# A sampled-convolution stream with another spacing of its stages: products 6 units ahead, copies 4 slots behind, 15 accumulators, 13 gather buffers

## The chip, the cores and the metric

The kernel runs on one core of a Trainium2 chip. The metric is the device time of one execution in microseconds (us); the median of the shown runs stands for a kernel. Engines are named as in the profile: PE (TensorE matmul), PEld (its weight loads), DVE (VectorE), ACT (ScalarE), POOL (GpSimd), SP (SyncE).

## What is computed

The input x has shape (2, 256, 128, 128), in float32. Two layers follow each other, each added to its input:

```
x = x + deform_conv(group_norm(x))      # layer 0
x = x + expert_conv(group_norm(x))      # layer 1
# deform_conv: a 3x3 convolution gives, for each pixel and each of 9 taps, an offset (dy, dx) and a mask;
# each tap samples x bilinearly at its moved position: four corners times four weights, times the mask;
# out = einsum('bckhw,ock->bohw', sampled, w_conv)   with c = o = 256, k = 9
# expert_conv: for 8 experts a 1x3 conv to 8 channels, then a 3x1 conv to 256, summed with probs
```

The part that matters here is the sampling of layer 0: 2 images x 128 rows x 9 taps = 2304 row samples of 128 pixels by 256 channels, and the products with `w_conv`.

## The kernel before

The head loads image 0, takes its norm and writes a table to device memory in which one line of 2 KB holds a pixel and the one below it, all 256 channels of each; two neighbouring lines, 4 KB in one piece, are the four corners of a cell. After the head comes the **stream**, which takes nearly all of the time, and then a tail with the second layer of image 1.

The stream works in **units**. A unit is one output row and one tap: 128 pixels on the partitions, four corners of 256 channels. Four rows (`CR`) form a chunk of 36 units (4 rows x 9 taps); two chunks form a group of 72 units, for which the sampling positions and weights are worked out together. There are 2304 units. The order of all instructions is written out by hand: a loop over **slots** `s` issues, in each slot, steps of several units at fixed distances. No scheduler moves anything; each engine runs its own instructions in the order in which the loop issues them, and waits where an operand or a buffer is not ready. In one slot:

- POOL issues `gather(s + GA)` (L567): one indirect DMA of 128 pieces of 4 KB, 512 KB, into a buffer `g` of the pool `gather`, which has `GA` buffers. The buffer is free once the last add of unit `s` has run.
- ACT runs `product(s + LP)` (L577): first corner times its weight into a new accumulator `acc` (pool `acc`).
- DVE runs three adds (L583): corners 1 and 2 of unit `s + 1` and corner 3 of unit `s`. After its corner 3 the unit's gather buffer is free.
- PE runs `apply_tap(s - LM)` (L608): one 128x512 product of the finished samples `sm` with `wcv` into `po`; four such steps, at the four units of a tap, make one tap complete. Two matmuls are issued for each of them.
- PE runs `turn(s - TL)` (L593): the accumulator of unit `s - 1` is transposed into `ptr` in PSUM (two halves). A `ptr` tile holds two units; there are three tiles. The accumulator is then free.
- ACT runs, in every other slot, `keep(s - TL - KL)` (L601): it copies a `ptr` tile of two units into `sm` (three tiles of four units).

At the end of a chunk DVE adds `po` to x (`residual`, L617) two slots after the last `apply_tap` of its half, then takes statistics (L621). `po` has one buffer for each half, so the first `apply_tap` of the next chunk waits for this add.

Other pieces lie in the same slots: the offset convolution of the group to come (`pu`, L335, and `om`, L350, on PE; its copy on ACT, its position arithmetic on DVE), over half of image 0's slots the table of image 1 (L667 and L677 on ACT, transposes on PE, loads and stores from SP), and over image 1's slots the second layer of image 0 (L766, L773, L832, L847, L856). Their slots are counted from the group's first unit; those of the offset pieces also from `GA`, those of the end of a chunk from `LM`.

Of the kernel before, what the change touches and what calls it, by code (L numbers as in the profile page):

```python
# [62 lines left out]
UPG = UPC * CPG  # L63
UPI = UPG * NG
UNITS = B * UPI
GA = 15
LP = 3
TL = 1
KL = 2
LM = 8  # L70
XB, XR = 3, 5


# [1 line left out]
def layers(ctx, tc, x, w_om, b_om, w_cv, b_cv, w_in, w_out, probs, out):  # L75
# [75 lines left out]
    def norm_pieces(stats, small, psum, tag, name):  # L151
        mean = cp.tile([P, NH], F32, name=f"mean_{name}")
        rstd = cp.tile([P, NH], F32, name=f"rstd_{name}")
        shift = cp.tile([P, NH], F32, name=f"shift_{name}")
        mv = small.tile([P, NH, 2], F32, tag="mv", name=f"mv_{name}")
        own = small.tile([P, NH], F32, tag="own", name=f"own_{name}")
        g = gavg.rearrange("p a b -> p (a b)")
        ps = {}

        def average(what):  # L160
            ps[what] = psum.tile([P, 512], F32, tag=tag, name=f"ps_{what}_{name}")
            nc.tensor.matmul(ps[what][:, :NH], lhsT=g, rhs=own, start=True, stop=True)

        def aggregate(h):
            nc.vector.bn_aggr(mv[:, h], stats[:, h].rearrange("p c s -> p (c s)"))

        pieces = [
            lambda: aggregate(0),
            lambda: aggregate(1),
            lambda: nc.vector.tensor_copy(own, mv[:, :, 0]),  # L170
            lambda: average("mean"),
            lambda: nc.vector.tensor_copy(mean, ps["mean"][:, :NH]),

            lambda: nc.vector.tensor_sub(own, own, mean),
            lambda: nc.vector.tensor_mul(own, own, own),
            lambda: nc.vector.tensor_add(own, own, mv[:, :, 1]),
            lambda: average("var"),
            lambda: nc.scalar.activation(rstd, ps["var"][:, :NH], AF.Sqrt, bias=eps),
            lambda: nc.vector.reciprocal(rstd, rstd),
            lambda: nc.vector.scalar_tensor_tensor(shift, mean, -1.0, rstd, ALU.mult, ALU.mult),  # L180
        ]
        return (mean, rstd, shift), pieces
# [100 lines left out]
    def pool(stack, name, bufs, **kw):  # L283
        return stack.enter_context(tc.tile_pool(name=name, bufs=bufs, reuse_waits="tile", **kw))
# [17 lines left out]
    stream = ExitStack()  # L302
# [217 lines left out]


    gp = pool(stream, "gather", GA)
    ap = pool(stream, "acc", 8)
    sp = pool(stream, "sampled", 3)
    st = pool(stream, "stat", 1)
    p_o = pool(stream, "p_o", 1, space=PSUM)
# [12 lines left out]
    def put(slot, piece, opens=False):  # L539
        sched[slot].append(piece)  # L540
        if opens:
            opened.add(slot)
# [20 lines left out]
    def gather(u):  # L563
        b, ci, k, r = unit(u)
        idx, _, rr, k = sample_of(u)
        gt = gp.tile([P, 2 * CELL], F32, tag="gt", name=f"g_{b}_{ci}_{k}_{r}")
        nc.gpsimd.indirect_dma_start(  # L567
            out=gt[:], out_offset=None, in_=tables[b][:, :],
            in_offset=bass.IndirectOffsetOnAxis(ap=idx[:, rr, k : k + 1], axis=0),
        )  # L570
        gts[u] = gt

    def product(u):
        b, ci, k, r = unit(u)
        _, wt, rr, k = sample_of(u)
        acc = ap.tile([P, C], F32, tag="acc", name=f"acc_{b}_{ci}_{k}_{r}")
        nc.scalar.activation(acc, gts[u][:, 0:C], AF.Copy, scale=wt[:, 0, rr, k : k + 1])  # L577
        accs[u] = acc

    def add(u, q):  # L580
        _, wt, rr, k = sample_of(u)
        gt = gts[u] if q < 3 else gts.pop(u)
        nc.vector.scalar_tensor_tensor(  # L583
            accs[u], gt[:, q * C : (q + 1) * C], wt[:, q, rr, k : k + 1], accs[u], ALU.mult, ALU.add
        )

    def turn(u):
        b, ci, k, r = unit(u)
        if r % 2 == 0:
            pts[u // 2] = p_t.tile([P, NH, 2 * W], F32, tag="t", name=f"ptr_{b}_{ci}_{k}_{r}")  # L590
        acc = accs.pop(u)
        for h in range(NH):
            nc.tensor.transpose(  # L593
                pts[u // 2][:, h, (r % 2) * W : (r % 2 + 1) * W], acc[:, h * P : (h + 1) * P], ident
            )

    def keep(u):
        b, ci, k, r = unit(u)
        if r == 1:
            sms[u // CR] = sp.tile([P, NH, N], F32, tag="sm", name=f"sm_{b}_{ci}_{k}")  # L600
        nc.scalar.copy(sms[u // CR][:, :, (r - 1) * W : (r + 1) * W], pts.pop(u // 2))  # L601

    def apply_tap(u):
        b, ci, k, i = unit(u)
        m, h = divmod(i, NH)
        if k == 0 and h == 0:
            pos_[b, ci, m] = p_o.tile([P, N], F32, tag=f"o{m}", name=f"po_{b}_{ci}_{m}")
        nc.tensor.matmul(  # L608
            pos_[b, ci, m], lhsT=wcv[:, h, k, m * P : (m + 1) * P], rhs=sms[u // CR][:, h],
            start=(k == 0 and h == 0), stop=(k == K2 - 1 and h == NH - 1),  # L610
        )
# [15 lines left out]
    def table_beside(b):  # L627
# [10 lines left out]
        def load_group(g, what):  # L638
            xt = held[what, "g", g] = x_tile(b, g, what)
            nc.sync.dma_start(xt, xv[:, :, g * GN : (g + 1) * GN])  # L640
            if g < XB:
                xts[b, g] = xt
# [42 lines left out]
        for j in range(NCH):  # L685
# [3 lines left out]
            elif i == 0:  # L689

                slot = max(slot, UPG * (g - NG + XR + 1) + LM + 12)
                put(slot, lambda g=g: load_group(g, "xs"))
# [9 lines left out]
        pieces, first_rows, last_rows = offset_pieces(b, oc, p_m, "m")  # L702
        at = UPI - 68 - GA - UPG + 46
        for n, piece in enumerate((*pieces[:2], *[None] * 3, *pieces[2:], first_rows)):
            if piece:
                put(at + 2 * n, piece)
        assert at + 2 * n < UPI - 68 - GA + 55
        put(UPI + UPI // 2, last_rows)
# [189 lines left out]
    def result_stats_of(b):  # L898
        stats1[b] = st.tile([P, NH, NCH, 6], F32, tag=f"stats{b}", name=f"stats1_{b}")

    result_stats_of(0)
    for G in range(B * NG):
# [6 lines left out]
        if (b, g) != (0, 0):  # L909
            for n, piece, opens in offsets_of(b, g):  # L910
                put(slot - 68 - GA + n, piece, opens)
    norms1 = [None] * B
    tabled = table_beside(1)
    assert tabled < UPI - GA - 16
    put(UPI - 16, sides.close)
    put(UPI, lambda: result_stats_of(1))
    slot = UPI + LM + 10
    norms1[0], pieces = norm_pieces(stats1[0], st, p_m, "m", "1_0")
# [12 lines left out]
    def when(u):  # L931
        return 0 <= u < UNITS

    s = min(sched)
    end = UNITS + LM
    while s < end or any(t >= s for t in sched):
        if when(s + GA):
            gather(s + GA)
        if when(s + LP):
            product(s + LP)  # L940

        order = [(s + 1, 1), (s, 3), (s + 1, 2)] if s in opened else [(s + 1, 1), (s + 1, 2), (s, 3)]
        for u, q in order:
            if when(u):
                add(u, q)
        if when(s - LM):
            u = s - LM
            apply_tap(u)
# [7 lines left out]
        if when(s - TL):  # L956
            turn(s - TL)
        if when(s - TL - KL) and (s - TL - KL) % 2 == 1:
            keep(s - TL - KL)
        for piece in sched.pop(s, ()):  # L960
# [67 lines left out]
```

## Time and profile before

| what | us |
|---|---|
| median of 3 runs (4056.10, 4062.48, 4065.21) | 4062.48 |
| the profiled execution, its own time | 4155.75 |
| its span, first to last instruction | 4154.0 |
| first and last gather issued | 156.2 and 3959.0 |

The profiled execution is 2.3% above the median of the runs; sums made in the profile are made against 4155.75 us. The stream's 2304 units take 3803 us between the first and the last gather, 1.65 us each. In a row of the profile, "idle before" is time in which that engine did nothing before such an instruction, with what ended most of it; a line "A <- B" in the list of waits adds up the idle time of A that the profile puts down to B.

### The profile page before, as it was taken

To read this page: it belongs to the slowest core of one execution; us is meant where nothing else is said; L and a number is where in the kernel's file an instruction comes from. 1 tells how busy PE (TensorE), PEld (TensorE's weight loads), DVE (VectorE), ACT (ScalarE), POOL (GpSimd) and SP (SyncE) were. 2 spreads that over 40 slices of the span, in tenths; PEclk is the share of its full clock that TensorE was granted. 3 is DMA by queue.
4 is the path that set the end of the run, shared out by engine and by line. 5 is a ranking of instruction groups with operands and counts; after the bars stand their busy time and mean duration, and the time that the engine had idled before them with its cause. 6 is when DMAs were issued, how large, how long until landed. Compare 5 with 4: busy or idle time off the path is not lost.

```text
span 4154.0 us, 51837 instructions
## 1 busy us (share of the span) xinstructions
PE 3497.9 (84%) x14044; PEld 1870.3 (45%) x14044; DVE 3442.1 (83%) x8066; ACT 1837.6 (44%) x3883; POOL 2335.4 (56%) x2388
## 2 busy tenths in 40 slices
PE   3588888888878888888889888889988889888889
PEld 2443434444444444444444444444545445444444
DVE  6488988888888887889788888888888888888887
ACT  2244444445444554444444444444444444444432
POOL 0356666656665666656566555556656556555531
PEclk9699999999999999989999999999999999999999
DMA  9999999999999999999889999999999999988835
GB/s 360 358 358 370 356 371 346 342 335 366 372 372 378 389 394 387 376 361 369 315 329 349 333 344 345 334 350 340 363 339 356 331 349 354 351 320 327 327 118 193
DMA packets 419516, 1425.46 MB, mean 343 GB/s; under 512 B 41582, under 2 KB 45338, under 8 KB 419098
## 3 DMA queue, kind: packets, MB, share of 16 engines
q0 software_dynamic: 331776, 1208.11, 78.0%
q1 hardware_dynamic: 87450, 214.04, 13.6%
q8 instruction: 114, 1.87, 0.2%
q14 instruction: 176, 1.44, 0.1%
HBM read 1298.20 MB, written 123.78 MB: 342 GB/s over the span
## 4 chain that ended last, share of the span: by engine, by line
PE 42%; DVE 25%; DMA 12%; issue 11%; another core or an unknown queue 6%; ACT 3%; POOL 1%; POOLq 1%; SPq 0%; ACTq 0%; DVEq 0%
PE po L608 23%; DVE acc L583 19%; DMA g<-table,cidx 9%; PE ptr L593 7%; PE pu L335 3%; PE pe L832 2%; PE ph L766 2%; DMA table<-hpx 2%; ACT acc L577 1%; PE ph L811 1%; PE pe L847 1%; DVE stats L621 1%; POOL g L567 1%; DVE x L617 1%
## 5 line engine op out<-in xcount | busy, mean ns | idle before, releaser
L583 DVE SCALAR_TENSOR_TENSOR acc<-g,wt,acc 128x256 f32<-128x256 f32 x6912 | 2961.8, 480 | 466.3 <-ACT acc L577 325.7
L567 POOL DMA_INDIRECT g<-table,cidx x2304 | 2284.5, 992 | 1530.9 <-DVE acc L583 556.5
L608 PE MATMUL po<-sm,wcv 128*128 128x512 f32 x4608 | 2502.1, 625 | 301.5 <-ACT sm L601 130.8
L601 ACT COPY sm<-ptr 128x512 f32<-128x512 f32 x1152 | 672.7, 584 | 1933.6 <-PE ptr L593 1096.3
L593 PEld LDWEIGHTS ptr<-idp,acc 128*128 128x128 f32 x4608 | 626.4, 146 | 1622.3 <-issue 1075.9
L593 PE MATMUL ptr<-idp,acc 128*128 128x128 f32 x4608 | 935.2, 286 | 195.4 <-ACT sm L601 76.3
L577 ACT ACTIVATE acc<-g,wt 128x256 f32<-128x256 f32 x2304 | 1060.1, 506 | 43.2 <-DMA g<-table,cidx 29.7
L608 PEld LDWEIGHTS po<-sm,wcv 128*128 128x128 f32 x4608 | 753.4, 199 | 375.3 <-ACT sm L601 160.4
L335 PE MATMUL pu<-wus,x 128*128 128x81 f32 (+2 forms) x1448 | 270.1, 313 | 7.8 <-issue 6.7
L335 PEld LDWEIGHTS pu<-wus,x 128*128 128x128 f32 x1448 | 216.8, 200 | 10.3 <-issue 6.9
L617 DVE SCALAR_TENSOR_TENSOR x<-po,bcv,x 128x512 f32<-128x512 f32 x116 | 86.3, 744 | 59.6 <-PE ptr L593 21.8
L832 PE MATMUL pe<-h,wout 128*128 128x256 f32 (+1 forms) x384 | 127.2, 461 | 1.0 <-DVE xc L856 1.0
L766 PE MATMUL ph<-xcn,win 128*64 128x254 f32 (+1 forms) x768 | 98.1, 403 | 4.6 <-issue 4.6
L856 DVE TENSOR_TENSOR xc<-pe,xc 128x512 f32<-128x512 f32 x76 | 49.8, 683 | 44.3 <-PE pe L847 20.0
L350 PE MATMUL om<-u,idp 128*128 128x216 f32 x192 | 56.0, 375 | 33.1 <-ACT u L344 30.7
L832 PEld LDWEIGHTS pe<-h,wout 128*128 128x128 f32 x384 | 67.9, 193 | 33.7 <-issue 30.1
L621 DVE BATCH_NORM_STATS2 stats<-x 128x6 f32<-128x512 f32 x116 | 79.2, 683 | 0.1
L766 PEld LDWEIGHTS ph<-xcn,win 128*64 128x64 f32 x768 | 55.9, 145 | 37.6 <-issue 16.6
L847 PE MATMUL pe<-h,wout 64*128 64x128 f32 (+1 forms) x752 | 70.1, 322 | 1.3 <-issue 1.3
L504 DVE COPY hpx<-hpt 128x512 f32<-128x512 f32 x32 | 21.1, 687 | 57.2 <-DMA table<-hpx 47.0
L799 DVE TENSOR_TENSOR v<-xcn 128x512 f32<-128x512 f32 x96 | 65.9, 744 | 1.8 <-ACT xcn L786 1.8
L847 PEld LDWEIGHTS pe<-h,wout 64*128 64x128 f32 x752 | 52.1, 187 | 27.4 <-issue 18.8
(115 smaller groups left out, 1019.3 us busy)
## 6 DMA issues: line engine op xcount, KB each, us to landing
g<-table,cidx POOLq DMA_INDIRECT x2304
table<-tpx SPq DMA_DIRECT2D x32, 1024.0 KB
table<-hpx SPq DMA_DIRECT2D x15, 2048.0 KB
x<-in_x_dram SPq DMA_DIRECT2D x29, 1024.0 KB
out_dram<-xc SPq DMA_DIRECT2D x38, 512.0 KB
x<-x SPq DMA_DIRECT2D x16, 1024.0 KB
out_dram<-x SPq DMA_DIRECT2D x26, 512.0 KB
xs<-in_x_dram SPq DMA_DIRECT2D x22, 512.0 KB
```

Source lines behind the costliest of these rows:

```text
L335: nc.tensor.matmul(held["ps", j][:, lo:hi], lhsT=xt[:, h, r * W : (r + 1) * W], rhs=w[:, lo - i + 2 : hi - i + 2], start=(i == 2 and h == ...
L567: nc.gpsimd.indirect_dma_start(out=gt[:], out_offset=None, in_=tables[b][:, :], in_offset=bass.IndirectOffsetOnAxis(ap=idx[:, rr, k : k + ...
L577: nc.scalar.activation(acc, gts[u][:, 0:C], AF.Copy, scale=wt[:, 0, rr, k : k + 1])
L583: nc.vector.scalar_tensor_tensor(accs[u], gt[:, q * C : (q + 1) * C], wt[:, q, rr, k : k + 1], accs[u], ALU.mult, ALU.add)
L593: nc.tensor.transpose(pts[u // 2][:, h, (r % 2) * W : (r % 2 + 1) * W], acc[:, h * P : (h + 1) * P], ident)
L601: nc.scalar.copy(sms[u // CR][:, :, (r - 1) * W : (r + 1) * W], pts.pop(u // 2))
L608: nc.tensor.matmul(pos_[b, ci, m], lhsT=wcv[:, h, k, m * P : (m + 1) * P], rhs=sms[u // CR][:, h], start=(k == 0 and h == 0), stop=(k == K ...
L617: nc.vector.scalar_tensor_tensor(v, pos_.pop((b, ci, m)), bcv[:, m : m + 1], v, ALU.add, ALU.add)
L621: nc.vector.bn_stats(stats1[b][:, m, ci], xts[b, ci // CPG][:, m, at_ : at_ + N])
L766: nc.tensor.matmul(o[:, :, to], lhsT=win[:, h, tap], rhs=pairs[:, t, :, of], start=(q == 0), stop=(q == 5),)
L832: nc.tensor.matmul(ps[t][:, m], lhsT=wout[:, 2 * t, m * P : (m + 1) * P], rhs=hs[ci], start=(banks or m == 0), stop=False,)
L847: nc.tensor.matmul(ps[t][:, m, to], lhsT=wout[half, 1, m * P : (m + 1) * P], rhs=hs[c][half, of], start=False, stop=(banks or m == NH - 1) ...
```

## The change

Five constants change: `GA`, `LP`, `KL`, `LM` and the number of buffers in the pool `acc`. Nothing is added or taken away: the same instructions run on the same engines, at other distances from each other.

```diff
-GA = 15
-LP = 3
+GA = 13
+LP = 6
 TL = 1
-KL = 2
-LM = 8
+KL = 4
+LM = 9
...
     gp = pool(stream, "gather", GA)
-    ap = pool(stream, "acc", 8)
+    ap = pool(stream, "acc", 15)
```


A gather buffer takes 4 KB of each partition and an accumulator 1 KB, so the two pools together take 67 KB in place of 68 KB. What the new distances mean for one unit u, counted in slots:

| step of unit u | slot before | slot after |
|---|---|---|
| gather issued (POOL), waits for the last add of unit | u - 15, unit u - 15 | u - 13, unit u - 13 |
| product (ACT), waits for the transposes of unit (its accumulator) | u - 3, unit u - 8 | u - 6, unit u - 15 |
| adds (DVE) | u - 1 and u | u - 1 and u |
| transposes (PE) | u + 1 | u + 1 |
| copy out of PSUM (ACT), u odd | u + 3 | u + 5 |
| its product with `wcv` (PE) | u + 8 | u + 9 |

Between the issue of a gather and the product that reads it lie 12 slots before and 7 after. Between the copy of the last two units of a tap and the tap's first `apply_tap` lie 2 slots before and 1 after. A `ptr` tile is wanted again by the transposes of the pair three pairs on; its copy lies 3 slots ahead of them before and 1 after.

## The prediction

> **What bounds the kernel now.** I read the page's part 1 and the groups first, then the list of waits, then one stall in the timeline, and last counted positions from the trace's start and end times.
>
> ```profile
> PE 3497.9 (84%) x14044; PEld 1870.3 (45%) x14044; DVE 3442.1 (83%) x8066; ACT 1837.6 (44%) x3883; POOL 2335.4 (56%) x2388
> L583 DVE SCALAR_TENSOR_TENSOR acc<-g,wt,acc 128x256 f32<-128x256 f32 x6912 | 2961.8, 480 | 466.3 <-ACT acc L577 325.7
> L608 PE MATMUL po<-sm,wcv 128*128 128x512 f32 x4608 | 2502.1, 625 | 301.5 <-ACT sm L601 130.8
> L601 ACT COPY sm<-ptr 128x512 f32<-128x512 f32 x1152 | 672.7, 584 | 1933.6 <-PE ptr L593 1096.3
> L593 PE MATMUL ptr<-idp,acc 128*128 128x128 f32 x4608 | 935.2, 286 | 195.4 <-ACT sm L601 76.3
> L577 ACT ACTIVATE acc<-g,wt 128x256 f32<-128x256 f32 x2304 | 1060.1, 506 | 43.2 <-DMA g<-table,cidx 29.7
> ```
>
> No engine is full: DVE and PE are both near 84%, and each idles some 500 us in the stream. ACT has less than half its time in work, yet DVE waits 325.7 us for ACT's products, and ACT itself stands 1933.6 us ahead of its PSUM copies. The products hardly wait for gathered data (29.7 us). So ACT is not slow and the data is not late; ACT stands at a copy, and products that it could have made lie behind it in its queue. The waits say it in pairs:
>
> ```profile
> ACT sm L601 <- PE ptr L593: 1096.3, 610, 9.5
> POOL g L567 <- DVE acc L583: 556.5, 794, 6.1
> DVE acc L583 <- ACT acc L577: 325.7, 79, 13.5
> PEld ptr L593 <- DVE acc L583: 263.1, 441, 2.1
> PEld po L608 <- ACT sm L601: 160.4, 59, 8.0
> PE po L608 <- ACT sm L601: 130.8, 53, 7.8
> PE po L608 <- DVE x L617: 90.0, 51, 5.4
> PE ptr L593 <- ACT sm L601: 76.3, 25, 5.0
> ```
>
> DVE's waits are few and long (79, 4.1 us each); PE's for DVE are many and short (441). One stall, in the timeline:
>
> ```profile
> 1148.39 0.59 ACT L601 COPY sm<-ptr 128x512 f32<-128x512 f32 x1 [5.75 <-PE ptr L593]
> 1148.87 0.91 ACT L577 ACTIVATE acc<-g,wt 128x256 f32<-128x256 f32 x2
> 1150.23 0.38 PE L593 MATMUL ptr<-idp,acc 128*128 128x128 f32 x2
> 1156.22 0.59 ACT L601 COPY sm<-ptr 128x512 f32<-128x512 f32 x1 [6.44 <-remote]
> 1156.86 2.07 PE L608 MATMUL po<-sm,wcv 128*128 128x512 f32 x2 [6.25 <-ACT sm L601]
> 1157.18 0.92 ACT L577 ACTIVATE acc<-g,wt 128x256 f32<-128x256 f32 x2
> 1157.74 4.42 DVE L583 SCALAR_TENSOR_TENSOR acc<-g,wt,acc 128x256 f32<-128x256 f32 x10 [5.18 <-ACT acc L577]
> ```
>
> ACT makes two products, then stands 6.44 us at a copy; DVE uses the products up and stops 5.18 us; PE stops for the copy. What holds the copy is not named by the profile ("remote"). By the trace's times (300 to 3900 us) DVE had 3.8 products in hand in the median and 6.5 at the 99th percentile, and led PE's transposes by 1.5 units in the median and 4.8 at the 99th.
>
> **The change, part by part.** No instruction is added or removed, so the sum is one of waits.
>
> *Products at LP 6.* DVE's slot s now needs ACT's slot s - 5 in place of s - 2: three more products stand in hand. Undisturbed, a unit takes DVE 1.31 us (12 adds in 5.33 us in the timeline), so that is 3.9 us of cover against a mean wait of 4.1 us: up to 326 us of DVE idleness can go. Fifteen accumulators let it: `product(s + 6)` needs the transposes of unit s - 9, where before `product(s + 3)` needed s - 5. Not all of the 326 us is time. At each chunk's end `residual` holds DVE to within two slots of PE (L617), as before. Counted by unit within the chunk, most of the long DVE stalls lie at units 20 to 35 and 0 to 4, ahead of this meeting, which comes at units 6 to 9 of the next chunk; what DVE gains there it partly hands back by waiting for PE. I take half: -163 us; both ends are 0 and -326.
>
> *Copies at KL 4, `apply_tap` at LM 9.* ACT may stand two slots further ahead of PE before a copy stops it, worth part of the same 326 us, not more. The price: PE's `po` is one slot behind the copy in place of two, and a `ptr` tile comes free two slots later. What hides it is ACT's lead over PE. Now PE waits 130.8 + 76.3 = 207 us in its matmul rows for this copy. The Trainium skill (PSUM — Partial Sum Buffer, Summary: rules for kernel authors) says "Evacuate promptly", which speaks against this. By the rule the 76.3 us of `ptr` waits would grow by the two lost slots in each of 25 waits, 25 x 2 x 1.65 = 83 us more, an estimate. By the row, ACT's copies wait 1096.3 us for PE: the copy is mostly ready before PE has delivered, and its slot is not what delays it. I take nothing for it, and keep 83 us for the range. ACT's other PSUM copies (L344, L677, L773) keep distances of two or three slots from their matmuls; they are late next, and cap ACT's lead there. One slot more at the end costs 1.65 us.
>
> *Thirteen gather buffers.* POOL's issue still waits for the add that frees the buffer. From that add to the landing of the gather in the same buffer the trace shows 6.8 us in the median, 10.2 at the 90th percentile, 14.7 at the 99th (by packets; landing is 4.9 us after the issue's end in the median). DVE needs the data 12 units later in place of 14: 12 x 1.31 = 15.7 us, so DVE itself is nearly always served. But ACT's product comes 7 slots after, and behind it in ACT's queue lie the copies, behind these PE's `po`. Shifting each measured landing and each product by the new distances, a third of the products would find no data yet, 1.9 us short on average; ACT then runs later than slot s, which it can as long as PE does not catch it. PE, at most one slot ahead of ACT, is touched where the landing takes over 7 x 1.31 = 9.2 us: about one unit in seven to ten. Bounds: 0, since ACT idles over half its time, and 230 units x 2 us / 4 (four gathers are in flight together, one late bunch is counted once) = 115 us. I take the middle, rounded: +60 us. DMA is not relieved either: it moves 343 GB/s in the mean and 410 to 430 in its fullest slices.
>
> *Position pieces.* Those counted from `GA` start two slots later, with the gathers they serve; end-of-chunk pieces one slot later with `LM`. SP's loads and stores and POOL's issues keep their distances to these. Nothing taken.
>
> Sum: 4155.75 - 163 + 60 + 1.65 = 4054.4 in the profile's terms. Against the median, 4062.48 / 4155.75 = 0.9776: 3963, I say 3965 us.
>
> A second rule was weighed: TensorE: Matmul & The Clock Gate, HAM oscillation: PE gaps over about 3.4 us let its clock drop. The row agrees in kind: the mean granted clock is 0.938, so at half speed for 0.124 of 4154 = 515 us, often just behind such a stall (the 1156.86 matmul pair takes 2.07 us, at other times 1.02). By the rule, fewer PE gaps would bring back up to 515 / 2 x 0.84 = 216 us more. I count none: the change lets DVE run on during a stall; PE stands still in it as before.
>
> **The rivals.**
>
> *Late gathers become the bound.* For: ACT executes in order, the copies now lie behind products whose gather was issued only 7 slots earlier, and while the table of image 1 is written the landing takes 7.3 us after the issue's start in the median, over 10 at the 90th. Against: 10 us of slack now. It decides from 9.2 us between add and landing. Price: the 115 us in full, and the gain cut to 60 us, as each late product also empties DVE's store: 4155.75 + 55 + 1.65 = 4212, x 0.9776 = 4118 us; without any gain 4176. Slower.
>
> *PE is the bound and takes all of it back.* DVE runs ahead, then waits the same time at `residual`: 4155.75 + 1.65, 4064 us, no change. For: PE stands in the same stalls. Against: 263 us of PE's weight loads waiting for DVE, which are time that PE could use.
>
> *All of DVE's waits go and half of the clock loss too.* 4155.75 - 326 - 108 + 1.65 = 3723, x 0.9776 = 3640 us at the far end; with two thirds of the 326 and no clock, 3852. For: stalls come in pairs, so one removed may spare the next. Against: `residual` and the other ACT copies.
>
> *The change doesn't do what it says.* With 13 buffers, ACT can't be six ahead while gathers take four units to land and one is in the add: 13 - 5 = 8 products in hand is the limit at 1.65 us a unit, above the 6 wanted; so it does.
>
> **How the numbers follow.** The forecast (3900 to 4045) has 0.42, the large gain 0.11, no change 0.09, late gathers and kindred losses 0.38; a little of the last lies above 4130. The low end leaves out part of the large gain, the high end part of the losses: 3870 to 4130. The forecast's own range is 3900 to 4045. Differences within 0.2% are about what a measurement of this kernel can't tell from none. Faster 0.53, same 0.09, slower 0.38.
>
> **What would show it.** Right: DVE's L583 wait for ACT falls from 325.7 us to under 120; L617's idle (59.6 us) rises; products in hand rise from 3.8 to 6 or more; ACT's L577 wait for DMA rises from 29.7 to some hundreds, without PE's wait for L601 (130.8 + 76.3) rising. Late gathers: L577's wait for DMA over 500 us together with PE's L601 waits over 300. No change: L617's idle grows by what L583's falls. The forecast is wrong if PE's L601 waits double, or if L583's wait for ACT stays above 250.

## The result and the profile after

The changed kernel takes 4233.24 us in the median (4219.36 to 4241.28, 4 runs), the kernel before 4059.45 us (4056.10 to 4065.21, 4 runs): a ratio of 1.0423, 95% interval [1.0388, 1.0458]. It is slower, beyond the range that was forecast, and on the other side. Its profiled execution took 4241.28 us (span 4239.6), 85.5 us more than the profiled one of before. The medians are 173.8 us apart: the profiled execution of before was 2.4% above this median, that of after 0.2%, so the two traces show about half of the loss.

The groups of the page after:

```profile
PE 3518.1 (83%) x14044; PEld 1899.0 (45%) x14044; DVE 3437.5 (81%) x8066; ACT 1892.2 (45%) x3883; POOL 2334.3 (55%) x2388
L583 DVE SCALAR_TENSOR_TENSOR acc<-g,wt,acc 128x256 f32<-128x256 f32 x6912 | 2957.5, 480 | 320.4 <-ACT acc L577 178.3
L608 PE MATMUL po<-sm,wcv 128*128 128x512 f32 x4608 | 2514.7, 628 | 336.3 <-issue 121.1
L577 ACT ACTIVATE acc<-g,wt 128x256 f32<-128x256 f32 x2304 | 1118.9, 507 | 966.2 <-DMA g<-table,cidx 714.3
L601 ACT COPY sm<-ptr 128x512 f32<-128x512 f32 x1152 | 662.2, 575 | 771.0 <-remote 430.9
L617 DVE SCALAR_TENSOR_TENSOR x<-po,bcv,x 128x512 f32<-128x512 f32 x116 | 86.6, 746 | 236.2 <-PE po L608 199.6
```

The last row was, before:

```profile
L617 DVE SCALAR_TENSOR_TENSOR x<-po,bcv,x 128x512 f32<-128x512 f32 x116 | 86.3, 744 | 59.6 <-PE ptr L593 21.8
```

The work is the same, the waits have moved. DVE waits 178.3 us for products in place of 325.7. But before `residual` (L617) it now idles 236.2 us, where it was 59.6: 147 us less at one place, 177 more at the other. On ACT the wait has gone from the copies (1933.6 us to 771.0) to the products (43.2 to 966.2), which now wait for gathered data. Of the list of waits:

```profile
ACT acc L577 <- DMA g<-table,cidx: 714.3, 677, 17.8
ACT sm L601 <- PE ptr L593: 273.7, 208, 7.9
PEld ptr L593 <- DVE acc L583: 228.6, 420, 2.1
DVE x L617 <- PE po L608: 199.6, 48, 12.0
PE po L608 <- ACT sm L601: 102.4, 37, 10.6
```

One stall of PE in the timeline of after, with the wait that follows it (start, busy time, engine, line; idle before in brackets; lines between these are left out):

```profile
2445.56 11.96 DVE L583 SCALAR_TENSOR_TENSOR acc<-g,wt,acc 128x256 f32<-128x256 f32 x27
2456.01 0.59 ACT L601 COPY sm<-ptr 128x512 f32<-128x512 f32 x1 [6.76 <-issue]
2456.65 2.08 PE L608 MATMUL po<-sm,wcv 128*128 128x512 f32 x2 [6.82 <-issue]
2470.10 0.75 DVE L617 SCALAR_TENSOR_TENSOR xt<-po,bcv,xt 128x512 f32<-128x512 f32 x1 [8.57 <-PE po L608]
2472.37 0.94 POOL L567 DMA_INDIRECT g<-table,cidx  x1 [7.49 <-DVE acc L583]
```

The forecast's cover works here: ACT and PE stand for 6.8 us and DVE adds on without a break. Then it stands 8.57 us at `residual`, because PE has not caught up, and POOL stands 7.49 us with it.

### The profile page after: what moved, and what is told of

Its sections match the earlier page's. It is cut to its first block, busy times and chain, and to the rows that moved or that the text cites. A ratio compares the mean times of both kernels' runs of the same rounds, so it can differ in the third digit from the quotient of the medians.

```text
span 4239.6 us, 51558 instructions
## 1 busy us (share of the span) xinstructions
PE 3518.1 (83%) x14044; PEld 1899.0 (45%) x14044; DVE 3437.5 (81%) x8066; ACT 1892.2 (45%) x3883; POOL 2334.3 (55%) x2388
## 4 chain that ended last, share of the span: by engine, by line
PE 36%; DVE 30%; issue 14%; DMA 11%; another core or an unknown queue 5%; ACT 2%; POOL 0%; SPq 0%; POOLq 0%; ACTq 0%; DVEq 0%
DVE acc L583 25%; PE po L608 20%; DMA g<-table,cidx 9%; PE ptr L593 6%; PE pu L335 2%; PE pe L832 2%; PE ph L766 2%; DMA table<-hpx 2%; PE pe L847 1%; PE ph L811 1%; ACT acc L577 1%; DVE stats L621 1%; DVE x L617 1%; DVE tstats L651 1%
## 5 line engine op out<-in xcount | busy, mean ns | idle before, releaser
L583 DVE SCALAR_TENSOR_TENSOR acc<-g,wt,acc 128x256 f32<-128x256 f32 x6912 | 2957.5, 480 | 320.4 <-ACT acc L577 178.3
L577 ACT ACTIVATE acc<-g,wt 128x256 f32<-128x256 f32 x2304 | 1118.9, 507 | 966.2 <-DMA g<-table,cidx 714.3
L593 PEld LDWEIGHTS ptr<-idp,acc 128*128 128x128 f32 x4608 | 639.3, 146 | 1620.6 <-issue 1129.1
L601 ACT COPY sm<-ptr 128x512 f32<-128x512 f32 x1152 | 662.2, 575 | 771.0 <-remote 430.9
L617 DVE SCALAR_TENSOR_TENSOR x<-po,bcv,x 128x512 f32<-128x512 f32 x116 | 86.6, 746 | 236.2 <-PE po L608 199.6
L766 PE MATMUL ph<-xcn,win 128*64 128x254 f32 (+1 forms) x768 | 115.7, 417 | 31.3 <-issue 30.5
L677 ACT COPY tpx<-tpt 128x512 f32<-128x512 f32 x64 | 37.2, 582 | 120.3 <-remote 46.8
L773 ACT ACTIVATE h<-ph,pr 128x256 f32<-128x256 f32 x32 | 15.2, 474 | 121.4 <-PE ptr L593 59.0
```

Source lines behind the costliest of these rows:

```text
L583: nc.vector.scalar_tensor_tensor(accs[u], gt[:, q * C : (q + 1) * C], wt[:, q, rr, k : k + 1], accs[u], ALU.mult, ALU.add)
L593: nc.tensor.transpose(pts[u // 2][:, h, (r % 2) * W : (r % 2 + 1) * W], acc[:, h * P : (h + 1) * P], ident)
L617: nc.vector.scalar_tensor_tensor(v, pos_.pop((b, ci, m)), bcv[:, m : m + 1], v, ALU.add, ALU.add)
L766: nc.tensor.matmul(o[:, :, to], lhsT=win[:, h, tap], rhs=pairs[:, t, :, of], start=(q == 0), stop=(q == 5),)
```

## The experiments

Ratios are to the kernel before on the same chip, with 95% intervals. The chips were not alike: on two of them the kernel before took 3702 us, on a third 4062 and 4139 us in two sessions; the runs of the result are of the second kind (4059 us). On the 3702 us chips the traces have no copy that starts over 0.5 us after its transposes, its tile and ACT were free; in the trace of before 218 of the copies between 300 and 3900 us do, 885 us together. These are stalls like the one shown in the prediction, for which the profile names no releaser.

The trace's semaphore events name one. The recorded end of a matmul is modelled; an update of PE's semaphore is the moment at which PE reported it. The copy at 1156.22 us in the prediction's stall starts 0.02 us after such an update (1156.20), while its transposes have their recorded end at 1150.61; and 212 of the 218 late copies start within 0.1 us of one. So ACT was held there by a late report of PE. In the ten traces of the third chip and of the result, 16 to 37% of PE's updates in the stream come over 0.5 us after the last recorded end of a matmul that sends one, the longest 15 us; in the ten traces of the 3702 us chips none does. Of ACT's and DVE's own updates in `before`, `after` and `lp_ga15` at most 1.1% come over 0.5 us late. (The stream is taken from 300 us to 3900, on the 3702 us chips to 3500.) The late copies are only one trace of this: `lp_ga15` and `stall_kl`, on the third chip, have no such copy, but 25% and 16% of late reports. Why PE reports late on one chip no record shows. "Where PE stalls" below means the chips with such late reports.

**The parts one by one** (the 3702 us chips).

`lp_only`: early products and the two pools, copies as before (the constants of the edits are written in one line here, against the kernel before).

```diff
-GA, LP, KL, LM = 15, 3, 2, 8     # acc 8
+GA, LP, KL, LM = 13, 6, 2, 8     # acc 15
```

> LP = 6 with GA = 13 and 15 accumulators, but KL = 2 and LM = 8 as before. Theory 1 (late gathers: ACT waits in order for data that was asked for only 7 slots earlier, and the PSUM copies behind it come late): nearly the whole loss is here, 4180 to 4240 us. Theory 2 (late copies: PE's po one slot behind the copy, ptr tiles freed two slots later): no loss here, 3980 to 4070 us.

3727.47 us against 3701.91: 1.0073 [1.0056, 1.0089]. Repeated beside the changed kernel:

> LP = 6 with GA = 13 and 15 accumulators, copies as before, once more. With PE's stalls: LP = 6 with GA = 15 gave 1.009 on such a chip; if late gathers add to it, 1.02 to 1.03; if the loss needs the late copies, 1.005 to 1.012. Without the stalls: 1.007, as measured.

1.0067 [1.0051, 1.0084]. A loss, small: theory 2, which put it all on the copies, misses; theory 1 has the sign but not the size.

`kl_only`: later copies alone.

```diff
-GA, LP, KL, LM = 15, 3, 2, 8
+GA, LP, KL, LM = 15, 3, 4, 9
```

> KL = 4 and LM = 9 alone, with GA = 15, LP = 3 and 8 accumulators as before. Theory 1: the gathers keep their 12 slots, so 4040 to 4080 us. Theory 2: the loss is here, 4180 to 4240 us.

3709.67 us, 1.0022 [1.0013, 1.0031]. Repeated:

> KL = 4 and LM = 9 alone once more. With PE's stalls: if the copies' smaller margin carries the loss, 1.02 to 1.04; if it is the two gather buffers or the products, under 1.01. Without the stalls: 1.002, as measured.

1.0021 [1.0014, 1.0029]. Alone, two slots later cost next to nothing.

`ga_only`: the two pools alone.

```diff
-GA = 15     # acc 8
+GA = 13     # acc 15
```

> GA = 13 and 15 accumulators alone, with LP = 3, KL = 2, LM = 8. Theory 1: 10 slots from issue to product are over the 90th percentile of the landing, so 4055 to 4090 us. Theory 2: as before, 4060 us. Theory 3 (the two gather buffers themselves carry the loss, because POOL and the DMA stop earlier when DVE stalls): 4150 us or more.

3703.76 us, 1.0005 [0.9997, 1.0014]. Repeated:

> GA = 13 and 15 accumulators alone once more. With PE's stalls: if the two gather buffers carry the loss (POOL stops earlier while DVE stands, and has less in store afterwards), 1.015 to 1.03; else under 1.005. Without the stalls: 1.0005, as measured.

1.0003 [0.9994, 1.0012]. Two gather buffers fewer cost nothing here by themselves. Theory 3 was about what they cost while DVE stalls; on a chip with late reports of PE they were not run alone, so there it stays untested.

The changed kernel itself, `after_3`:

> The changed kernel beside its parts on one chip. If the kernel before takes over 4000 us here, PE's long stalls are there and the ratio is 1.035 to 1.045, as on the two chips so far; if it takes about 3700 us, the parts add up without them: 1.010 to 1.015.

3749.90 us against 3702.11: 1.0127 [1.0110, 1.0143]. `lp_only` has the two pools in it, so the parts give 0.67 + 0.21 = 0.9%: they cost more together than apart. For a trace close to the kernel before on such a chip `ga_only` serves. Its groups first, then those of `after_3`:

```profile
L583 DVE SCALAR_TENSOR_TENSOR acc<-g,wt,acc 128x256 f32<-128x256 f32 x6912 | 2961.8, 480 | 141.0 <-ACT acc L577 75.1
L617 DVE SCALAR_TENSOR_TENSOR x<-po,bcv,x 128x512 f32<-128x512 f32 x116 | 86.3, 744 | 7.2 <-PE po L608 7.0
```

```profile
L583 DVE SCALAR_TENSOR_TENSOR acc<-g,wt,acc 128x256 f32<-128x256 f32 x6912 | 2956.1, 480 | 97.7 <-ACT acc L577 30.6
L617 DVE SCALAR_TENSOR_TENSOR x<-po,bcv,x 128x512 f32<-128x512 f32 x116 | 86.3, 744 | 80.7 <-PE po L608 80.5
```

DVE is the busiest engine in `after_3` (92%, PE 89%). It saves 43 us before its adds and loses 74 at `residual`: 30 us of the 49 between the two spans (3699.9 and 3749.1), read off two rows. PE comes late to the meeting.

**Which margin of the copy counts.** `lm10`: the changed kernel, with `po` again two slots behind the copy.

```diff
-LM = 9
+LM = 10
```

> The changed kernel with LM = 10: po is again two slots behind the copy; the ptr tiles are still freed two slots later than before. Theory 1: a late copy has one slot more before PE feels it, so a part of the loss goes: 4140 to 4210 us. Theory 2, if the po margin is what counts: 4050 to 4110 us; if the ptr tiles are what counts: unchanged, 4230 us.

3744.41 us, 1.0121 [1.0104, 1.0138]: no recovery. (The times expected of these first four runs were those of a 4060 us chip; what tells is the ratio.) The waits show why, `after_3` first:

```profile
PEld po L608 <- ACT sm L601: 230.3, 219, 5.0
PE po L608 <- ACT sm L601: 131.5, 136, 3.2
PE ptr L593 <- ACT sm L601: 42.6, 55, 2.9
```

and `lm10`:

```profile
PEld ptr L593 <- ACT sm L601: 618.2, 626, 7.0
PE ptr L593 <- ACT sm L601: 206.2, 216, 6.6
```

PE no longer waits for the copy at `po`, but at the `ptr` tile that the same late copy has not freed. It is the copy that is late, not one of its readers that is too close.

**The same distances where PE stalls.** The changed kernel again, on the third chip:

> The changed kernel once more, beside runs of the kernel before on the same chip. The kernel before has taken 4059 us in the runs of the result and 3702 us on the chip of the single-part runs, where no copy waited without a cause that the trace shows. If the loss comes from the distances alone, the ratio is 1.04 on any chip. If most of it needs the long stalls of PE that the first chip shows, the ratio on a chip at 3700 us is near the sum of the parts, 1.007 + 0.002: 1.005 to 1.015.

4297.68 us against 4138.87: 1.0384 [1.0344, 1.0423], as in the result. `lp_ga15`: early products, but with fifteen gather buffers and eight accumulators.

```diff
-LP = 3
+LP = 6
```

> LP = 6 alone, with GA = 15 and 8 accumulators (KL = 2, LM = 8). Theory 1 (late gathers): 9 slots from issue to product in place of 7, so at least two thirds of the 0.7% that LP = 6 with GA = 13 loses are gone: ratio 1.000 to 1.003. If it is the place of the copy behind an earlier product, or the accumulators, the loss stays or grows: 1.007 or more.

4173.91 us, 1.0093 [1.0065, 1.0122]: a quarter of the loss. The numbers expected were for the other chip, so this does not decide as it was meant to. In its trace the eight accumulators tie ACT's products to PE, and DVE's wait for products is down to 176.0 us all the same (325.7 in the trace of before), without any gain in time:

```profile
ACT acc L577 <- PE ptr L593: 1122.0, 1001, 9.3
DVE acc L583 <- ACT acc L577: 176.0, 73, 8.1
```

**Stalls put in by hand.** In each of the 64 chunks PE waits for a DMA that starts only when PE has come there:

```diff
+        if u % UPC == 28:
+            to = pts[u // 2][0:16, 0, 0:P]
+            nc.tensor.matmul(to, lhsT=late, rhs=ident, start=True, stop=True)
+            nc.sync.dma_start(late, w_cv[:, 0, 0, 0:16])
+            nc.tensor.matmul(to, lhsT=late, rhs=ident, start=True, stop=True)
```

The transposes overwrite what these two matmuls leave. Into the kernel before and the changed one (third chip):

> The kernel before, with one stall of PE put into each chunk, at the transposes of its unit 28: a small matmul, then a DMA that overwrites its weights, then a second matmul that waits for the DMA. PE stands about 3 to 6 us, 64 times. If DVE's three products in hand are what PE's stall uses up, the loss is most of 64 x 4 us: 150 to 300 us more than the kernel before. If the coupling hides it, under 100 us.

> The changed kernel with the same stalls. The forecast's step (three more products in hand cover a stall) says: less loss than stall_before, so its ratio to stall_before is at least 0.02 below that of the two kernels without stalls. The theory that PE's stall is only handed on to the meeting of DVE and PE at the chunk's end, with the loss of the distances on top: ratio to stall_before as large as without stalls or larger, 1.01 to 1.04.

`stall_before` 4376.42 us, 1.0593 [1.0545, 1.0640]; `stall_after` 4543.47 us, 1.0978 [1.0932, 1.1024]. The stall adds 237.6 us to the kernel before (4376.42 - 4138.87) and 245.8 us to the changed one (4543.47 - 4297.68). Its size in `stall_before`, and what DVE then waits for (the lines lie lower in that file: L585 is the add, L579 the product, L597 the second small matmul):

```profile
DVE acc L585 <- ACT acc L579: 528.3, 142, 11.7
PE ptr L597 <- DMA late<-in_w_cv_dram: 429.7, 58, 16.4
```

About 7 us each; the trace puts the waits of PE's matmuls for that tile at 458.8 us in all, and at 549.5 us in `stall_after`. About half of it is time, in both kernels. The ratio of the two is 1.036 with the stalls and 1.038 without, where the forecast's step wanted it at least 0.02 lower: the changed kernel pays no less for a stall of PE, however far DVE runs on. (A cover of under some 30 us in all would lie within the intervals.)

Once more on the same chip, with the parts:

> The kernel before with one stall of PE in each chunk, as in stall_before. On a chip at 3700 us, where DVE is 92% busy: if PE's room there hides a stall, the loss is under 100 us (ratio under 1.027); where PE's own stalls lie beside it (over 4000 us) it was 237 us, 1.059.

> The changed kernel with the same stalls. If PE's stalls are what turns 1.3% of loss (chip at 3700 us) into 4% (chips over 4000 us), its ratio to stall_before_2 is clearly over 1.0127 on a chip at 3700 us: 1.025 to 1.045. If the stalls are not what does it, 1.010 to 1.016. If three more products in hand cover a stall, under 1.005.

> KL = 4 and LM = 9 alone, with the stalls. Against stall_before_2: 1.00 to 1.005 if the late copies cost no more with stalls than without (1.002); 1.015 or more if they are what the stalls make dear.

> LP = 6, GA = 13 and 15 accumulators with the copies as before, with the stalls. Against stall_before_2: 1.005 to 1.010 if the early products cost no more with stalls than without (1.007); 1.02 or more if late gathers behind a stall are what is dear; under 1.000 if the products in hand pay off as soon as there are stalls.

| kernel, all with the stalls | us | ratio to before (4062.05) |
|---|---|---|
| `stall_before_2` | 4292.98 | 1.0582 [1.0550, 1.0614] |
| `stall_kl` (KL 4, LM 9) | 4298.43 | 1.0592 [1.0566, 1.0617] |
| `stall_lp` (LP 6, GA 13, acc 15) | 4386.73 | 1.0796 [1.0767, 1.0826] |
| `stall_after_2` | 4448.00 | 1.0964 [1.0935, 1.0993] |

Against `stall_before_2`, by these ratios, that is 0.1% for the later copies, 2.0% for the early products with 13 buffers and 3.6% for both. The added stalls have not raised the loss above the 3.8% that this chip shows without them; since the chip has stalls of its own, these runs can't tell whether stalls are what turns 1.3% into 3.8. But where PE stalls anyhow, the early products cost three times what they cost at 3702 us, and the later copies, harmless alone, add another 1.5% on top of them. How much of the 2.0% is the 13 buffers' was not run: `lp_ga15`, with fifteen and without added stalls, lost 0.9%.

**What joins the two.** Count, for the copy of unit u, the last product ahead of it in ACT's queue: unit u + 1 + KL + LP. Its gather could be issued only after the last add of unit u + 1 + KL + LP - GA, that is u - C with C = GA - LP - KL - 1. Two kernels with C = 5, one without early products and one with them and an earlier copy:

```diff
-GA, LP, KL, LM = 15, 3, 2, 8     # acc 8
+GA, LP, KL, LM = 13, 3, 4, 9     # acc 15: ga13_kl4
+GA, LP, KL, LM = 13, 6, 1, 8     # acc 15: lp6_kl1
```

> GA = 13, 15 accumulators, KL = 4, LM = 9, but LP = 3: no early products. The measured losses fall in the order of one number, GA - LP - KL - 1: how many units before the copied one the add lies that frees the gather buffer of the last product in front of the copy in ACT's queue. Before 9, KL alone 7, GA alone 7, LP alone with GA = 15 6, LP alone with GA = 13 4, changed 2. Here it is 5. If this number sets the loss: between KL alone and LP alone, 1.004 to 1.006 on a chip at 3700 us and 1.010 to 1.020 on one over 4000 us. If the early products themselves carry the loss: the sum of KL alone and GA alone, 1.0025 at 3700 us, 1.001 to 1.005 over 4000 us.

> LP = 6, GA = 13, 15 accumulators, LM = 8, and the copies one slot earlier, KL = 1: the number is 5 again, with early products. If the number sets the loss: the same as ga13_kl4 within 0.3%, and under LP = 6 with KL = 2 (1.007 at 3700 us, 1.020 beside added stalls). If the early products carry the loss: as LP = 6 with KL = 2 or more, and at least 0.4% above ga13_kl4.

`ga13_kl4` 3709.68 us, 1.0021 [1.0012, 1.0030]; `lp6_kl1` 3711.66 us, 1.0027 [1.0017, 1.0038], both against 3702.21. With C, and from each trace the time from the end of a pair's transposes to the start of its copy, and the share of taps whose first `po` matmul starts within 0.15 us of the copy's end, so that PE stood ready:

| kernel (3702 us chips) | C | loss | copy after transposes, median us | PE stood ready |
|---|---|---|---|---|
| `ga_only` | 7 | 0.05% | 0.75 | 13% |
| `kl_only` | 7 | 0.22% | 1.47 | 17% |
| `ga13_kl4` | 5 | 0.21% | 2.97 | 23% |
| `lp6_kl1` | 5 | 0.27% | 2.28 | 30% |
| `lp_only` | 4 | 0.73% | 2.58 | 32% |
| changed (`after_3`) | 2 | 1.27% | 4.57 | 41% |
| `lm10` | 2 | 1.21% | 5.06 | 0% (held at `ptr` first) |

That early products as such carry the loss is refuted: with the copy one slot earlier (KL 1 for 2) two thirds of `lp_only`'s 0.73% are gone. That C alone sets it is half right: the two kernels with C = 5 agree, but `ga13_kl4` lies below the range expected and no higher than `kl_only` with C = 7; the larger losses begin under 5. How late the copies are does not order the losses by itself: `ga13_kl4`'s copies come later than `lp_only`'s, at a third of the loss. And KL moves a second distance along with C, that from the copy to the `ptr` tile's next use (4 slots in `lp6_kl1`, 3 in `lp_only`), which no run here separates. No kernel here is faster than the one before.

## Why the prediction was wrong

- *Products at LP 6: -163 us.* The size of the wait was right (DVE's wait for ACT fell by 147 us, of 326 at most; products in hand rose from 3.8 to 5.8), the step "I take half" was not. All of it came back at `residual`, +177 us. The stalls are PE's, not ACT's: the prediction read in its timeline that PE stops for the copy, but the copy was waiting for PE's report. The forecast itself says that PE stands still in them as before, and yet counts DVE's freed time as time. Between 300 and 3900 us PE has as many gaps of over 3 us in its matmul records after as before (45 and 46), and they are longer, 273 us together in place of 225. The stall runs show the price: about half of PE's standing time is lost in both kernels. The rival "PE is the bound and takes all of it back", given 0.09, was right on this term, and its sign came true; the loss came on top.
- *Copies at KL 4: nothing.* Alone this holds (1.002; 1.001 beside the stalls). Together with LP 6 it fails. I named the cover, ACT's lead over PE, and did not ask what the other half of the change does to it: with products waiting 714.3 us for data, ACT has that lead no more. The row I leaned on, 1096.3 us of copies waiting for PE, became 273.7. The Trainium skill's "Evacuate promptly" (PSUM — Partial Sum Buffer, Summary: rules for kernel authors) had the sign (`kl_only` lost 0.2%), though the page gives PSUM's size as its reason and not a queue; my estimate by it, 83 us, was for the `ptr` tiles alone.
- *Thirteen gather buffers: +60 us.* The third of the products without data was foreseen (677 waits in 2304 products, 29%), and PE's margin of 9.2 us as the deciding point too. The term counted the product's distance, 7 slots, and not that of the copy behind it in ACT's queue, C = 2. At 3702 us the losses follow C well enough to make this the likely reason that it was too small; on the chips with late reports it was not measured by itself. This was the rival on the slower side, given 0.38 and 4118 us, 4176 without any gain; the run took 4233.
- *The clock.* I counted nothing; the mean granted clock fell from 0.938 to 0.923 in the two traces. The rule of TensorE: Matmul & The Clock Gate (HAM oscillation) agrees in kind: time at half speed rises from 0.124 of 4154 to 0.154 of 4240 us, 515 to 653 us, by the same count as in the prediction. By its working (half of the difference, times PE's busy share) that is some 57 us of PE's work, an estimate; what it cost in time no run separates.
- *Signs named beforehand.* L583's wait for ACT did not fall under 120 (178.3), L577's wait for DMA passed 500 (714.3), but PE's waits for L601 in its matmul rows fell (102.4 + 63.8 us, from 207), which I had set as the mark against late gathers. On a chip with stalls that mark is masked, since a stall too ends in a copy; at 3702 us the `po` row rises from 61.4 (`ga_only`) to 131.5 (`after_3`). Neither of the two signs that were to prove the forecast wrong came, since both looked at waits for ACT and neither at `residual`.

Left open: why PE reports late on the one chip, and why the same distances cost three times as much there. That PE is the engine that binds there, while DVE does at 3702 us and hides part of PE's loss, fits the stall runs, but was not tested by itself. Of the 3.6 to 4.2% about a third is what the same distances cost at 3702 us (1.27%); the rest is located (early products, and later copies on top of them), not explained.

## What to carry to other kernels

On an engine that executes in order, a step's slack is that of the slowest thing ahead of it in its queue: two lags that cost little alone (0.2% and 0.7% here) add up to one distance (here GA - LP - KL - 1), and that sum has to be worked out when buffers are moved. A store in front of an engine covers a stall only if the engine that stalled has room to catch up before the two meet again; look for the next meeting (here `residual`, every 36 units) and ask who is late there. Before a stall is made the ground of a forecast, ask whether it belongs to the kernel or to the chip, and compare the recorded end of the work with the moment at which its semaphore was updated.

## What the runs showed of the hardware

The kernel before took 3702 us on two chips, with a granted clock of 0.979 to 0.984 in its runs, and 4062 and 4139 us in two sessions on a third, with 0.946 to 0.949 and 0.936 to 0.942. Data moves no slower there: in the four such traces without added stalls a gather lands 4.9 to 5.1 us after the end of its issue in the median, on the 3702 us chips it takes 5.8 to 6.1 us, at 379 to 384 GB/s over the span in place of 329 to 342. What comes late is PE's report: 16 to 37% of its semaphore's updates over 0.5 us after the recorded end, none on the 3702 us chips, with ACT's and DVE's updates on time. In the prediction's stall five of PE's updates come together, from 1156.20 to 1156.47 us, while the last five recorded ends of matmuls that send one lie between 1146.49 and 1150.61. That looks as if the report was held and not the work, which is not shown.
